# Attention scores computed with the keys on partitions, on one Trainium2 core

## The chip, the cores and the metric

The kernel runs on one core of a Trainium2 chip. A core has five engines that run their own instruction streams and wait for one another through semaphores: TensorE (PE in the profile, its weight loads PEld), VectorE (DVE), ScalarE (ACT), GpSimd (POOL) and SyncE (SP), which here issues all the DMAs. The metric is the device time of one execution in microseconds, the median of several. Before the change it was 720.5 us, the median of three runs (719.56 to 722.37).

## What is computed

One transformer block with cross attention, in fp32. The eight sequences of 256 tokens and 512 features are taken with a context of the same shape; 16 heads of 32 features; an MLP of 2048 inner features. The mask is all ones.

```python
x = layer_norm(hidden_states, ln1_w, ln1_b)
q = (x @ q_w + q_b)                      # -> B, H, LQ, HD
k = (encoder_hidden_states @ k_w + k_b)
v = (encoder_hidden_states @ v_w + v_b)
scores = einsum('bhqd,bhkd->bhqk', q, k) / sqrt(HD)
scores = where(mask, scores, finfo.min)
attn = softmax(scores, axis=-1)
out = einsum('bhqk,bhkd->bhqd', attn, v) @ cproj_w + cproj_b
hidden = out + residual
y = gelu(layer_norm(hidden, ln2_w, ln2_b) @ fc_w + fc_b) @ proj_w + proj_b
return hidden + y
```

## The kernel before

The sequences are worked in two groups of four (`g` = 0, 1). Each projection is a product of 2x2 blocks done with seven products instead of eight (`quad`; the two MLP layers nest this twice, `grown` and `grown2`), so the matrix engine's products alternate with sums and differences of blocks: `plus` and `minus` on DVE or POOL, evictions from PSUM in `take` on ACT or DVE. Results of the projections k, q and v go to DRAM (`kd`, `qd`, `vd`) and come back by unit.

A unit of attention is one sequence and one set of four heads: 32 units. `scores` (L818) loads `ku`, `qu` and `vu`, and issues eight products `s`, 32 rows deep, four heads side by side on the rows of the array. Queries lie on the 128 partitions and 256 keys along the row. For each of the eight tiles of 128x256 a DVE instruction (`max`, L841) adds the mask, scales, writes the tile to `pr` in SBUF and leaves the row's maximum in `st`; an ACT instruction (L847) takes the exponential with that maximum as bias and leaves the row's sum. DVE then takes the reciprocals of the eight sums (L851), transposes them (L854), and two DMAs carry them through DRAM into `r` (`rd`, L505, and back by L499), spread over the 32 partitions of each head. `attend` (L862) runs `LOOK` = 2 units later: 16 transposes of 128x128 on TensorE (`turn`, L870) bring the keys onto partitions, four evictions of 128x512 (`pt`, L512) bring them back to SBUF, eight products `av` multiply by `vu`, and `att` (L532) multiplies by `r` on DVE.

The instruction order of all engines is fixed before anything runs, by a planner in the kernel itself (`Order`). Each operation has a list of engines that can do it with a cost for each (`alts`), and a due time `vt`, worked back from the windows (`WINDOWS`) in which each stream of matrix products is to run. `run` then steps through time and gives every free engine the ready operation with the earliest due time, if a buffer is free. Buffers are slots: `Q` of 1024 columns (two `P` of 512), `H` of 256, PSUM banks `W` for products and `C` for scores and transposes. Operations marked `lock` on DVE and POOL are kept from running at the same time in the plan. DMAs are modelled with a fixed delay and eight lanes. Each engine then executes its list strictly in order.

The streams run in the order: projections of group 0, attention of group 0 (`core0`) mixed with the projections of group 1 and sums of MLP weights (`fw`, `pw`), attention of group 1 (`core1`) mixed with the output projection and the first MLP layer of group 0, and then the output projection of group 1 and the rest of the MLP (`pr0`, `fc1`, `pr1`).

Of the kernel before, what the change touches and what calls it, by code (L numbers as in the profile page):

```python
# [19 lines left out]
FLT_MAX = 3.4028234663852886e38  # L20


SLOTS = {"Q": (45, 1024), "P": (36, 512), "H": (13, 256), "sm": (10, 32), "st": (8, 32), "MB": (4, 256)}
# [3 lines left out]


READY = {"PE": 0.24, "DVE": 0.16, "ACT": 0.18, "POOL": 0.2, "SP": 0.0}
BORROW = 25.6  # L30
SWITCH = 0.0

AHEAD = {"PE": 1000.0, "DVE": 66.7, "ACT": 36.8, "POOL": 25.4, "SP": 26.9}

DMA_FIXED, DMA_RATE, DMA_LANES = 3.0, 0.34, 8
# [10 lines left out]
class Op:  # L46
    __slots__ = (
        "n", "alts", "fn", "deps", "users", "vt", "bufs", "name", "mode", "table", "mb", "start",
        "end", "eng", "stream", "waiting", "ready", "lead", "slack", "psum_of", "after", "lock",
# [3 lines left out]
class Order:  # L53
# [9 lines left out]
    def op(self, name, alts, reads, writes, fn, mode=None, table=None, mb=0.0, lead=0.0, lock=False):  # L63
        o = Op()
        o.n, o.alts, o.fn, o.name, o.mode, o.table, o.mb = (
            len(self.ops), alts, fn, name, mode, table, mb,
        )
        o.lock = lock
        o.deps, o.users, o.vt, o.bufs, o.lead = set(), [], None, [], lead
        o.start = o.end = o.eng = None  # L70
        o.stream, o.psum_of = self.now, None
        o.after = self.streams[self.now][-1] if self.streams[self.now] else None
        for b, keys in reads:
            for k in keys if keys is not None else range(b.keys):
                if k in b.writers:
                    o.deps.add(b.writers[k])
                    if b.kind in BANKS and b.writers[k].alts[0][0] == "PE":
                        o.psum_of = b.writers[k]
                b.readers.setdefault(k, []).append(o)
            if b not in o.bufs:  # L80
                o.bufs.append(b)
        for b, keys in writes:
            for k in keys if keys is not None else range(b.keys):
                if k in b.writers:
                    o.deps.add(b.writers[k])
                for r in b.readers.get(k, []):
                    o.deps.add(r)
# [3 lines left out]
        o.deps.discard(o)  # L91
# [9 lines left out]
    def times(self, windows):  # L101
        pe = lambda o: o.alts[0][0] == "PE"
        for name, ops in self.streams.items():
            if not ops:
                continue
            t0, tm, t1 = windows[name]
            total = sum(o.alts[0][1] for o in ops)
            at = 0.0
            for o in ops:
                f = 2.0 * at / total  # L110
                o.vt = t0 + (tm - t0) * f if f < 1.0 else tm + (t1 - tm) * (f - 1.0)
                at += o.alts[0][1]
        cost = lambda o: min(a[1] for a in o.alts) + READY[o.alts[0][0]] + (
            DMA_FIXED + 1.0 + o.mb / DMA_RATE if o.alts[0][0] == "SP" else 0.0
        ) + o.lead
        for name, (t0, tm, t1) in windows.items():
            back = [o for o in self.ops if o.stream == name and not pe(o)]
            if name not in self.streams or self.streams[name]:
                continue
            for i, o in enumerate(back):  # L120
                o.vt = t0 + (t1 - t0) * i / len(back)
# [3 lines left out]
        for o in reversed(self.ops):  # L125
            if not pe(o):
                c, early = [u.vt for u in o.users], o.vt
                o.vt = (min(c) if c else (o.after.vt if o.after else 0.0) + 20.0) - cost(o)
                if o.psum_of is not None:
                    o.vt = min(o.vt, o.psum_of.vt + 1.2)  # L130
                if early is not None:
                    o.vt = min(o.vt, early)
# [4 lines left out]
    def run(self):  # L137
        ops = self.ops
        free_slots, pending = {}, {}
        for kind, (n, _) in SLOTS.items():  # L140
            free_slots[kind] = [(0.0, i) for i in range(n)]
        for kind, n in BANKS.items():
            free_slots[kind] = [(0.0, i) for i in range(n)]
        pairs = [[0.0, 0.0] for _ in range(SLOTS["Q"][0])]
        free_slots["Q"] = free_slots["P"] = None
        bufs = []
        seen = set()
        for o in ops:
            for b in o.bufs:
                if id(b) not in seen:  # L150
                    seen.add(id(b))
                    bufs.append(b)
        for b in bufs:
            b.left = len(b.ops)
            b.vt = min(o.vt for o in b.ops)
            if b.kind in free_slots:
                pending.setdefault(b.kind, []).append(b)
        for kind in pending:
            pending[kind].sort(key=lambda b: b.vt)
        vts = {kind: [b.vt for b in bs] for kind, bs in pending.items()}  # L160

        light = lambda b: b.kind == "C" and b.name.startswith("ps_") and not b.name.startswith("ps_pt")
        vts["heavy"] = [b.vt for b in pending.get("C", []) if not light(b)]
        engines = ["PE", "DVE", "ACT", "POOL", "SP"]
        at = dict.fromkeys(engines, 0.0)
        cands = {e: [] for e in engines}
        for o in ops:
            o.waiting = len(o.deps)
            o.ready = 0.0
        def offer(o):  # L170
            for e, _ in o.alts:
                cands[e].append(o)
        for o in ops:
            if not o.waiting:
                offer(o)
        port = 0.0
        lanes, n_dma = [0.0] * DMA_LANES, 0
        order, mode, table, lag, dma_at = [], None, None, 0.0, 0.0
        busy = dict.fromkeys(engines, 0.0)
        self.trace = []  # L180

        def room(o, t):

# [1072 lines left out]
```

## Time and profile before

| | |
|---|---|
| median of three runs | 720.5 us (719.56 to 722.37) |
| span of the profiled execution, first to last instruction | 718.6 us |
| instructions | 13,665 |
| TensorE clock granted, mean | 0.997 of full speed |
| moved by DMA | 144.06 MB, 200 GB/s over the span |
| last product `av` of the attention, start | 409.0 us |
| last `att` | 409.5 us, 0.4 us long |

The profiled execution's time apart from its span is not listed; the span lies 1.9 us below the median of the runs. "Busy" is the union of an engine's instructions; on DVE and ACT neighbours overlap by some tens of ns, so the mean length of an instruction is a little more than what it takes from its engine. In a group of instructions the columns are line, engine, operation, output and inputs with their shapes, count, then busy time and mean ns of one, then the idle time of the engine before them and what ended it. In a list of stretches, each engine has its busy microseconds and its number of instructions. In a timeline the columns are start, length, engine, line and operation; an `x3` at the end means that three neighbours are shown as one.

### The profile page before, as it was taken

What the parts mean: (1) busy time and instruction counts of PE and PEld (TensorE: products, weight loads), DVE (VectorE), ACT (ScalarE), POOL (GpSimd) and SP (SyncE); (2) the same over time, 40 slices, a digit from 0 to 9 for tenths busy, and PEclk for the clock granted to TensorE, in tenths of its full rate; (3) what the DMA queues carried; (4) which work ended last, traced back from release to release, by engine and by line L of the source; (5) the groups of instructions that cost most, each with busy time, mean ns of one, the idle gap of its engine ahead of it and who ended that gap; (6) DMA issues with size and microseconds to landing.
All of it is one profiled execution on the core that took longest, in us unless ns stands there. A gap on an engine that the chain in (4) does not pass through costs nothing.

```text
span 718.6 us, 13665 instructions
## 1 busy us (share of the span) xinstructions
PE 699.8 (97%) x4753; PEld 563.0 (78%) x4753; DVE 592.1 (82%) x1382; ACT 294.5 (41%) x829; POOL 281.3 (39%) x261
## 2 busy tenths in 40 slices
PE   6999999998999999999999999999999999998997
PEld 5555675566755687877788799999989988897997
DVE  2889589987898889888988867996579898997992
ACT  2243278657576656745659840120000107610000
POOL 1383046581563700030104588364677004843000
PEclk9999999999999999999999999999999999999999
DMA  7968875998789855274534743468666557730741
GB/s 232 327 205 313 306 252 183 283 337 283 206 281 317 278 183 169 78 219 146 161 94 143 256 123 100 148 204 245 183 180 182 160 157 246 278 103 1 247 150 59
DMA packets 119332, 144.06 MB, mean 200 GB/s; under 512 B 14136, under 2 KB 82272, under 8 KB 119264
## 3 DMA queue, kind: packets, MB, share of 16 engines
q1 hardware_dynamic: 119264, 143.19, 62.7%
q8 instruction: 38, 0.62, 0.4%
q14 instruction: 30, 0.25, 0.1%
HBM read 98.59 MB, written 44.56 MB: 199 GB/s over the span
## 4 chain that ended last, share of the span: by engine, by line
PE 90%; DVE 6%; DMA 2%; issue 1%; SPq 0%; POOL 0%; DVEq 0%; POOLq 0%
PE fc_X L541 13%; PE pr_X L541 13%; PE ps_pt L870 7%; PE fc_W L541 7%; PE pr_W L541 7%; PE s L541 5%; PE av L541 4%; PE k_X L541 4%; PE o_X L541 4%; PE q_X L541 4%; PE v_X L541 3%; PE fc_Y L541 3%; PE pr_Y L541 3%; PE o_W L541 2%; PE q_W L541 2%; PE v_W L541 2%
## 5 line engine op out<-in xcount | busy, mean ns | idle before, releaser
L847 ACT ACTIVATE pr<-pr,st 128x256 f32<-128x256 f32 x256 | 127.4, 502 | 82.3 <-DVE st L841 80.8
L841 DVE CUSTOM_DVE_ANT_0 pr<-s,mb 128x256 f32<-128x256 f32 x256 | 92.4, 418 | 10.1 <-PE s L541 9.9
L1030 ACT ACTIVATE h<-h,cols 128x256 f32<-128x256 f32 x128 | 54.3, 499 | 55.7 <-DVE h L532 52.7
L870 PEld LDWEIGHTS ps_pt<-ident,pr 128*128 128x128 f32 x512 | 59.4, 141 | 18.5 <-issue 5.6
L870 PE MATMUL ps_pt<-ident,pr 128*128 128x128 f32 x512 | 70.1, 275 | 2.4 <-DVE st L841 1.9
L532 DVE TENSOR_TENSOR h<-fc_X,h 128x512 f32<-128x512 f32 x80 | 54.3, 685 | 8.3 <-PE fc_X L541 8.1
L512 ACT COPY pt<-ps_pt 128x512 f32<-128x512 f32 x88 | 49.1, 579 | 24.6 <-PE ps_pt L870 20.5
L847 ACT ACTIVATION_READ_ACCUMULATOR pr<-pr,st 128x1 f32 x256 | 48.9, 191 | 0.0
L532 DVE TENSOR_TENSOR h<-fc_W,h 128x512 f32<-128x512 f32 x48 | 32.9, 686 | 5.3 <-PE fc_W L541 3.7
L541 PE MATMUL s<-ku,qu 32*128 32x256 f32 x512 | 36.9, 400 | 0.0
L541 PE MATMUL av<-pt,vu 128*32 128x256 f32 x512 | 35.0, 385 | 0.0
L541 PEld LDWEIGHTS s<-ku,qu 32*128 32x128 f32 x512 | 23.4, 184 | 13.5 <-issue 12.0
L512 ACT COPY e<-pr_X 128x256 f32<-128x256 f32 x4 | 1.5, 373 | 76.7 <-PE pr_X L541 76.7
L532 POOL TENSOR_TENSOR h<-h,fl 128x512 f32<-128x512 f32 x8 | 11.1, 1396 | 55.5 <-DVE fl L532 54.9
L541 PEld LDWEIGHTS av<-pt,vu 128*32 128x32 f32 x512 | 14.3, 109 | 20.1 <-issue 6.6
L532 DVE TENSOR_TENSOR po<-pr_X,po 128x256 f32<-128x256 f32 x40 | 16.7, 417 | 14.3 <-PE pr_X L541 14.3
L512 DVE COPY pt<-ps_pt 128x512 f32<-128x512 f32 x40 | 26.8, 683 | 1.8 <-PE ps_pt L870 1.1
L841 DVE DVE_READ_ACCUMULATOR2_ANT st<- 128x1 f32 x256 | 21.0, 82 | 0.0
L649 POOL TENSOR_TENSOR rs_y<-rs_y,neg_half 128x2 f32<-128x2 f32 x8 | 6.7, 836 | 35.8 <-DVE rs_y L646 35.7
L530 POOL TENSOR_TENSOR z0t<-h,h 128x512 f32<-128x512 f32 x12 | 15.0, 1272 | 13.3 <-PE fc_X L541 11.6
L530 POOL TENSOR_TENSOR z0i<-z0t,z0t 128x512 f32<-128x512 f32 x10 | 16.4, 1660 | 6.3 <-DVE y1t L532 3.3
L532 DVE TENSOR_TENSOR att<-av,r 128x256 f32<-128x256 f32 x32 | 13.4, 418 | 6.5 <-PE av L541 3.9
(643 smaller groups left out, 1841.7 us busy)
## 6 DMA issues: line engine op xcount, KB each, us to landing
fl<-prd SPq DMA_DIRECT2D x21, 256.0 KB
fl<-fcd SPq DMA_DIRECT2D x19, 256.0 KB
fw<-in_L_xattn_fc_w_dram SPq DMA_DIRECT2D x16, 256.0 KB
ku<-kd SPq DMA_DIRECT2D x32, 128.0 KB
vu<-vd SPq DMA_DIRECT2D x32, 128.0 KB
qu<-qd SPq DMA_DIRECT2D x32, 128.0 KB
r<-rd SPq DMA_DIRECT2D x32, 128.0 KB
pw<-in_L_xattn_proj_w_dram SPq DMA_DIRECT2D x32, 128.0 KB
```

What stands on the lines that cost most here:

```text
L512: (nc.scalar.copy if e == "ACT" else nc.vector.tensor_copy)(to(), of_())
L530: nc.gpsimd.tensor_tensor(to()[:, ts(k, 512)], in0()[:, ts(k, 512)], in1()[:, ts(k, 512)], op)
L532: E[e].tensor_tensor(to(), in0(), in1(), op)
L541: nc.tensor.matmul(o(), l(), r(), start=first, stop=True, skip_group_check=True)
L649: lambda e, rs=rs: nc.gpsimd.tensor_tensor(tile_of(rs)[:, 2:4], tile_of(rs)[:, 0:2], neg_half[:, 0:2], ALU.pow), lock=True)
L841: nc.vector.tensor_tensor_reduce(at(p_, pk), at(sb[j], i), tile_of(mb), scale=-SCALE, scalar=FLT_MAX, op0=ALU.add, op1=ALU.min, accum_out= ...
L847: nc.scalar.activation(at(p_, pk), at(p_, pk), AF.Exp, bias=tile_of(st)[:, 8 + c : 9 + c], scale=-1.0, accum_out=tile_of(st)[:, 16 + c : 1 ...
L870: nc.tensor.transpose(at(ps, 2 * kc + i, 1, P), at(pr[j // 2], 2 * (j % 2) + i)[:, ts(kc, P)], ident.t)
L1030: lambda e, f=f, b=b, c=c: nc.scalar.activation(at(h[f][b], c), at(h[f][b], c), AF.Gelu_apprx_tanh, bias=col(c_fcb + f * 4 + c), scale=1.0 ...
```

## The change

In the new program the scores of a unit come with the keys on partitions: `ku` is loaded into the array and `qu` moves. Nothing is transposed by TensorE. The scale goes into the weight and bias of the first layer norm and the bias of `q`, where `cols` is made, and the mask becomes a bias per partition, so a plain eviction (`take` with a bias, ACT or DVE) brings each of the eight score tiles to `pr`. The maximum over the keys now runs across partitions: two DVE reductions of 128x1024 (`mx`) reduce blocks of 32x32 that they transpose on the way, six small DVE instructions (`fold`) fold the four groups of 32 partitions into one, a DMA stores the 32x32 result to DRAM (`md`), and another brings it to all 128 partitions (`mm`, 128x1024, 512 KB). `less` subtracts it (POOL or DVE, two instructions of 128x512 for each half), ACT takes the exponential of 128x1024, twice per unit, and `ss` adds the two blocks of keys (DVE or POOL, 128x512, twice). `attend` adds four products of `ss` with a tile of ones to the eight of `av`, so that the sums over the keys stand beside the result in the same bank on 32 partitions per head; DVE takes their reciprocal and multiplies.

```diff
-        mm(f"s{u}", 0.97, [(q, None), (k, None)], [(s, None) for s in sb], [
-            (lambda i=i, j=j: at(sb[j], i), lambda i=i, j=j: tile_of(q)[j * HD : (j + 1) * HD, ts(i, P)],
-             lambda j=j: tile_of(k)[j * HD : (j + 1) * HD, :], True)
-            for i in range(2) for j in range(4)], mode="row")
+        row = lambda t, j: tile_of(t)[j * HD : (j + 1) * HD]
+        mm(f"s{u}", 1.076, [(q, None), (k, None)], [(s, None) for s in sb], [
+            (lambda kc=kc, j=j: at(sb[j], kc), lambda kc=kc, j=j: row(k, j)[:, ts(kc, P)], lambda j=j: row(q, j), True)
+            for kc in range(2) for j in range(4)], mode="row")
         pr = [Buf(f"pr{u}_{h}", "Q", 4) for h in range(2)]
-        st = Buf(f"st{u}", "st", 24)
...
-                    nc.vector.tensor_tensor_reduce(
-                        at(p_, pk), at(sb[j], i), tile_of(mb), scale=-SCALE, scalar=FLT_MAX, op0=ALU.add, op1=ALU.min,
-                        accum_out=tile_of(st)[:, 8 + c : 9 + c])
...
+        for kc in range(2):
+            for j in range(4):
+                take(f"ev{u}_{j}{kc}", (pr[j // 2], [2 * (j % 2) + kc]), (sb[j], [kc]), lambda j=j, kc=kc: at(pr[j // 2], 2 * (j % 2) + kc),
+                     lambda j=j, kc=kc: at(sb[j], kc), 256, lambda kc=kc: col(2 * (4 * g + b) + kc))
+        mx = Buf(f"mx{u}", "mx", 3)
+        for h in range(2):
+            T.op(f"mx{u}_{h}", [("DVE", 1.14)], [(pr[h], None)], [(mx, [h])], lambda e, h=h: nc.vector.tensor_reduce(
+                tile_of(mx)[:, 32 * h : 32 * h + 32], tile_of(pr[h]).rearrange("p (n r) -> p n r", r=32), axis=mybir.AxisListType.X,
+                op=ALU.max, apply_transpose=True))
+
+        def fold(e):
+            t = tile_of(mx)
+            part = lambda i, n=P: t[:n, 64 + 32 * i : 96 + 32 * i]
+            two = t[:, 0:64].rearrange("p (j k q) -> p j k q", j=4, k=2)
+            v = nc.vector
+            v.tensor_tensor(part(0).rearrange("p (j q) -> p j q", j=4), two[:, :, 0, :], two[:, :, 1, :], ALU.max)
+            v.transpose(part(1), part(0))
+            v.tensor_copy(part(2, 64), part(1)[64:128])
+            v.tensor_tensor(part(3, 64), part(1, 64), part(2, 64), ALU.max)
+            v.tensor_copy(part(4, 32), part(3, 64)[32:64])
+            v.tensor_tensor(part(5, 32), part(3, 32), part(4, 32), ALU.max)
+        T.op(f"fold{u}", [("DVE", 0.6)], [(mx, [0, 1])], [(mx, [2])], fold)
+        md = dram(f"md{u}", [32, 32])
+        store(f"md{u}", md, None, [(mx, [2])], lambda: md.t, lambda: tile_of(mx)[:32, 224:256], 0.01)
+        M = Buf(f"mm{u}", "Q")
+        load(f"mm{u}", M, None, lambda: tile_of(M), lambda: md.t.rearrange("a r -> (a r)").partition_broadcast(P), 0.5, src=[(md, None)])
+        ss = Buf(f"ss{u}", "Q", 2)
+        for h in range(2):
+            def less(e, h=h):
+                for i in range(2):
+                    j = 2 * h + i
+                    p_ = at(pr[h], i, 1, 512).rearrange("p (k q) -> p k q", k=2)
+                    E[e].tensor_tensor(p_, p_, at(M, j)[:, None, :].to_broadcast([P, 2, S]), ALU.subtract)
+            T.op(f"less{u}_{h}", [("POOL", 2.315), ("DVE", 1.21)], [(pr[h], None), (M, None)], [(pr[h], None)], less, lock=True, pieces=2)
+            T.op(f"exp{u}_{h}", [("ACT", 0.88)], [(pr[h], None)], [(pr[h], None)],
+                 lambda e, h=h: nc.scalar.activation(tile_of(pr[h]), tile_of(pr[h]), AF.Exp), table="exp")
...
-                        nc.tensor.transpose(at(ps, 2 * kc + i, 1, P), at(pr[j // 2], 2 * (j % 2) + i)[:, ts(kc, P)], ident.t)
...
         av = Buf(f"av{u}", "C")
+            (lambda j=j: tile_of(av)[j * HD : (j + 1) * HD, 256:512], lambda: ones, lambda j=j: at(ss, j), True)
+            for j in range(4)] + [
...
+        T.op(f"r{u}", [("DVE", dve(256))], [(av, None)], [(R, None)], lambda e: nc.vector.reciprocal(tile_of(R), tile_of(av)[:, 256:512]))
```

The rest of the change is in the planner and at the start. The planner's model is finer: a delay for each pair of engines (`TAIL`), separate costs for entering and leaving the narrow modes of the array, DMAs with a base and a service time by name, a two-part POOL operation that lets DVE's sums in between its parts (`pieces`), new due times (`WINDOWS`, `LEADS`), and `LOOK` = 3. All instructions of all engines therefore come in another order. At the start, 14 small products on a tile of ones (`WARM`) run on TensorE before any data are there, the context of group 0 is loaded by quarters (`token_quarters`: 256 columns of two row blocks at a time, instead of whole rows), and the masks come as 16 rows beside the bias rows instead of eight broadcasts.

```diff
-LOOK = 2
+LOOK = 3
+WARM = 14
...
+    for _ in range(WARM):
+        nc.tensor.matmul(first[:64, :64], warm, warm, start=True, stop=True, skip_group_check=True)
...
-        ct = token_tiles(g, "c", ef)
+        ct = token_quarters(g, "c", ef) if g == 0 else token_tiles(g, "c", ef)
...
+            halves = o.lock and e == "POOL" and o.pieces == 2
             if o.lock and (e == "DVE" or e == "POOL"):
-                port = t + dur
+                port = t + (dur / 2 if halves else dur)
```

More of the change, by code (lines that the diff above doesn't have):

```diff
@@ L152, in run @@
                     bufs.append(b)
+        light = lambda b: b.name.startswith("ps_") and not b.name.startswith("ps_pt")
+        vts = {k: [] for k in free}
+        vts["heavy"] = []
         for b in bufs:
@@ L155, in run @@
             b.vt = min(o.vt for o in b.ops)
[L156 to L166, printed above, removed]
-        for o in ops:
[L168 to L172, printed above, removed]
+            if b.kind in free:
+                vts[b.kind].append(b.vt)
+                if b.kind == "C" and not light(b):
+                    vts["heavy"].append(b.vt)
+        for v in vts.values():
+            v.sort()
+        at = dict(START)
+        cands = {e: [] for e in ENGINES}
+        for o in ops:
+            o.waiting, o.ready = len(o.deps), 0.0
         for o in ops:
             if not o.waiting:
[L175 to L180, printed above, removed]
+                for e, _ in o.alts:
+                    cands[e].append(o)
+        port, lanes, n_dma, dma_at = 0.0, [0.0] * DMA_LANES, 0, 0.0
+        order, mode, table, lag, second = [], None, None, 0.0, None
+        skip = dict.fromkeys(ENGINES, -1.0)
+        before = lambda k, last: bisect.bisect_left(vts[k], last)
         def room(o, t):
@@ L345, in run @@
[L345 to L353 removed]
+            done(o, o.end + AFTER[e])
+        self.span = max(o.end + AFTER[o.eng] for o in ops)
         return sorted(order, key=lambda o: (o.start, o.n))
```

498 lines of the change are left out of this document (252 added, 246 removed).

## The prediction

> **What bounds the kernel now.** I read the page's busy times first, then its chain of waits, then the busy time of each engine in two stretches, cut at the end of the last attention product (409.9 us).
>
> ```profile
> PE 699.8 (97%) x4753; PEld 563.0 (78%) x4753; DVE 592.1 (82%) x1382; ACT 294.5 (41%) x829; POOL 281.3 (39%) x261
> ...
> PE 90%; DVE 6%; DMA 2%; issue 1%; SPq 0%; POOL 0%; DVEq 0%; POOLq 0%
> ```
>
> ```profile
> core 0: us, PE busy (x) PEld busy (x) DVE busy (x) ACT busy (x) POOL busy (x), PEclk, DMA share, GB/s
> 0.00:18.00 18.00, 11.77 (x54) 9.26 (x55) 5.30 (x7) 4.70 (x7) 2.48 (x16) 1.00 0.71 233
> 0.00:94.30 94.30, 88.02 (x365) 54.90 (x368) 66.06 (x153) 31.75 (x76) 30.91 (x43) 1.00 0.83 279
> ...
> 0.00:409.90 409.90, 400.60 (x2616) 280.45 (x2617) 339.69 (x1006) 244.23 (x717) 147.70 (x166) 1.00 0.71 228
> 409.90:718.60 308.70, 299.16 (x2139) 282.52 (x2137) 252.46 (x378) 50.32 (x113) 133.62 (x96) 0.99 0.53 164
> ```
>
> PE is busy for 400.6 of the first 409.9 us and holds 90% of the chain, so TensorE bounds the attention stage. But DVE is busy for 339.7 us of the same stretch, 83%: there are only 70 us of room on the engine to which the change gives most of its new work. ACT (60%) and POOL (36%) have more. The second stretch holds what the change leaves alone: output projection, MLP, no scores.
>
> **What it takes from TensorE.** These are pieces of the chain, in order of time (start, length, what).
>
> ```profile
> 97.63 1.08 PE s L541 x16
> ...
> 104.49 1.00 PE av L541 x16
> ...
> 108.87 1.75 PE ps_pt L870 x16
> ```
>
> The 16 transposes of one unit cost 1.75 us; 32 units give 56.0 us, all removed. The scores keep shape and count (keys instead of queries are the loaded side), so 1.08 us stays. `av` gains four products with ones to its eight, each of the same moving width: half of 1.00 us more, 16.0 us in all. The issue order of the changed program also puts 24 fc products of 128x256 behind the last `av` that stood ahead of it; the chain has four such products (eight records) in 1.73 us:
>
> ```profile
> 290.13 1.73 PE fc_X L541 x8
> ```
>
> so 10.4 us move from the first stretch to the second. PE's work up to the last `av` is then 400.6 - 56.0 + 16.0 - 10.4 = 350 us. If TensorE still set the pace, the whole would be 718.6 - 56.0 + 16.0 = 678.6 us of span.
>
> **What it gives to DVE.** I count what the changed program issues on DVE up to the last `att`, and price it from start to start, because neighbours overlap by some 0.08 us.
>
> ```profile
> 200.04 0.42 DVE L841 CUSTOM_DVE_ANT_0 pr<-s,mb 128x256 f32<-128x256 f32 x1
> ...
> 201.07 1.29 DVE L512 COPY pt<-ps_pt 128x512 f32<-128x512 f32 x2
> 202.28 0.68 DVE L532 TENSOR_TENSOR xt<-q_Y,xt 128x512 f32<-128x512 f32 x1
> 202.88 2.39 DVE L532 TENSOR_TENSOR x1t<-x,x 128x1024 f32<-128x1024 f32 x1
> 205.19 0.19 DVE L851 RECIPROCAL st<-st 128x8 f32<-128x8 f32 x1
> 205.41 0.21 DVE L854 STREAM_TRANSPOSE tr<-st 128x32 f32<-128x32 f32 x1
> 205.55 0.38 DVE L532 TENSOR_TENSOR att<-av,r 128x256 f32<-128x256 f32 x1
> ```
>
> ```profile
> 450.50 3.49 DVE L532 TENSOR_TENSOR z0t<-h,z0t 128x1024 f32<-128x1024 f32 x3
> 453.90 1.22 DVE L532 TENSOR_TENSOR z0i<-z0t,z0t 128x1024 f32<-128x1024 f32 x1
> ```
>
> Between 200.04 and 201.07 lie three maxima: 0.343 us for 256 columns. Two copies of 512 take 202.28 - 201.07: 0.605 each. Three sums of 1024 take 3.40: 1.133 each. A small instruction that waits for the one before it starts 0.22 us after it (205.41 - 205.19).
> Removed: 256 maxima (87.8), 40 copies of transposed blocks (24.2), 32 reciprocals with their transpose (0.36 each, 11.5), three mask rows (0.8): 124.3 us. The other 88 copies, and the accumulator reads, leave ACT.
> Added: 77 of the 256 evictions with the mask bias (26.4; the other 179 are ACT's); 64 maxima of transposed blocks over 128x1024, at the 1024 price (72.5); 192 instructions of `fold`, six to a unit, each waiting for the one before (42.2); 32 reciprocals of 128x256, at the 0.418 of `att`, since `att` waits for each (13.4); 46 subtractions (27.8) and 29 sums (17.5) of 512. Together 199.8 us. In the rest of DVE's list up to the last `att` some 27 instructions fewer stand there: -13.
> So DVE's work up to the last `att` is 339.7 - 124.3 + 199.8 - 13 = 402 us, against PE's 350. The order of the two has turned round: this is the step on which the forecast rests.
>
> Three prices have no row. The maximum with its transposition may carry the longer tail of the small transpose (0.21 against 0.14 to the next start): at most 0.07 x 64 = 4.5 us more; below 1.133 I see no reason. `fold` could run packed like an accumulator read, 0.082 us, if its waits cost nothing: 192 x 0.082 = 15.7 in place of 42.2. I take 0.22, since a reciprocal and a transpose of the same tile are the same pattern. The third is the meeting with POOL:
>
> ```profile
> 201.66 2.53 POOL L530 TENSOR_TENSOR x1t<-x,x1t 128x512 f32<-128x512 f32 x2
> ```
>
> DVE's `x1t` from 202.88 took 2.39 us, not 1.22: POOL's second half ended at 204.19, and 2.39 is the rest of it and then a full 1.1. So an instruction with two SBUF inputs waits for a POOL instruction in progress. What that costs on the average shows in the groups of such sums:
>
> ```profile
> L532 DVE TENSOR_TENSOR z1t<-h,h 128x1024 f32<-128x1024 f32 x8 | 12.1, 1542 | 0.0
> L532 DVE TENSOR_TENSOR z1t<-h,z1t 128x1024 f32<-128x1024 f32 x8 | 10.2, 1281 | 0.0
> L532 DVE TENSOR_TENSOR z1i<-z1t,z1t 128x1024 f32<-128x1024 f32 x7 | 9.6, 1366 | 0.0
> L1183 DVE TENSOR_TENSOR hid<-hid,pb 128x1024 f32<-128x1024 f32 x7 | 8.5, 1215 | 0.0
> ```
>
> Their weighted mean is 1355 ns against 1215 for the undisturbed: 0.14 us each. The 75 new subtractions and sums add 75 x 0.14 = 11 us at the present share of POOL. Below, nothing, if the new order keeps the two apart; above, the rival on POOL. I take 11.
> [...]
>
> **The sum.** DVE idles for 12.7 of the first 18 us (18.00 - 5.30), before any data are there, and later for
>
> ```profile
> DVE st L851 <- ACT pr L847: 2.8, 5, 1.2
> DVE kws L532 <- DMA ct<-in_L_xattn_k_w_dram: 2.7, 1, 2.7
> DVE att L532 <- DMA r<-rd: 2.6, 1, 2.6
> ```
>
> some 8 us that have nothing to do with PE's pace. I keep both. The first stretch is 402 + 11 + 12.7 + 8 = 434 us; PE sits idle for 84 us of it. The second is 308.7 + 10.4 = 319.1, TensorE's as now, since DVE's load there hardly changes. Span 753. The span of this profile, 718.6, lies 1.9 us under the median of the runs, 720.5; with that, 755 us.
> The start (tokens in quarters, 14 idle products ahead) I price at nothing: it can at most shorten the 6 us for which PE waits for its first tiles, and with DVE ahead in load that does not reach the end in full. ACT's new work (64 exponentials of 1024, 179 evictions) replaces 256 shorter ones with reads and 88 copies, and stays under its 60%.
>
> **The rivals.**
> TensorE stays the bound (faster). For it: a third of the new subtractions alone are DVE's, and DVE can be kept from POOL by order. Against it: even with `fold` packed and no meeting at all DVE needs 402 - 26.5 - 101 x 0.14 = 361 us, plus 20.7 idle: 382, still above 350. That gives 382 + 319.1 + 1.9 = 703 us; TensorE alone gives 678.6 + 1.9 = 681. I take 692. Chance 0.24.
> POOL and DVE block each other (slower still). POOL takes 82 halves of subtractions and 35 sums, at
>
> ```profile
> L530 POOL TENSOR_TENSOR z0t<-h,h 128x512 f32<-128x512 f32 x12 | 15.0, 1272 | 13.3 <-PE fc_X L541 11.6 <-PE pr_W L541 1.5
> ```
>
> 149 us, less 38 us of other sums that leave POOL's list ahead of the last `att` at the same prices: 259 in the stage instead of 147.7, so a meeting is 1.75 times as likely. The 170 long sums and the five instructions of each `fold` that read two inputs or copy in SBUF then lose 330 x 0.14 x 1.75 = 81 us instead of the 25 counted (0.14 for each of 101 + 75): 755 + 56 = 811. It decides once meetings are as frequent as by chance; against it, the planner holds each of the two back while a sum of the other runs, `fold` excepted. Chance 0.14.
> The broadcast comes late. It carries 32 x 512 KB, 12.6 MB more than `r` did; at the 349 GB/s of the fullest stretch that is 36 us of the queue, and it now stands before the exponentials, not behind them. For it:
>
> ```profile
> 59.00:62.00 3.00, 3.00 (x22) 1.48 (x21) 3.00 (x10) 0.69 (x1) 0.00 (x0) 1.00 0.95 349
> ...
> 152.44 7.24 DMA r<-rd
> ```
>
> and DMA busy for 0.83 of the first 94 us. Against it: three units are under way instead of two, some 25 us. If eight units waited 7.24 us each, on a DVE otherwise undisturbed: 703 + 58 = 761. Chance 0.08.
> In between the costs cancel: 720, chance 0.04.
>
> **How the numbers follow.** The forecast, DVE as the bound of the attention stage, has 0.50 and 755 us; its own range, from the low price of `fold` (728) to twenty us more of meetings, is 728 to 775. Faster: 0.24 and a little of the middle, 0.25. Within 0.5%, which is about what these runs can tell from no change: 0.05. Slower: 0.70. The range of 695 to 795 leaves out the better part of the first rival and most of the second, about 2 in 10.
>
> **What would show it.** Right: PE's busy share in the first stretch falls to some 80% with waits for DVE (`pr`, `mx`, `att`), DVE at 95%, the last `av` after 420 us, `fold` near 1.3 us a unit, and about 319 us after the last `av`. Wrong: PE still over 95% before the last `av`, which comes before 390 us; or PE waiting for `mm` DMAs; or POOL instructions of 512 well over 1.27 us.

## The result and the profile after

The changed kernel takes 872.0 us (median of four runs, 869.8 to 876.3), against 720.5 before: 1.210 times as long, with an interval of 1.205 to 1.214. The forecast was 755 us with a range to 795, so the sign was right and the size was not: it is 117 us over the forecast, outside its range. The profiled execution has a span of 871.3 us, and its own time was 873.1.

From the page, the busy times and the shares of the chain of waits (in per cent of the span):

```profile
PE 722.7 (83%) x4525; PEld 545.7 (63%) x4525; DVE 769.2 (88%) x1166; ACT 261.7 (30%) x489; POOL 447.3 (51%) x375
...
PE 29%; DVE 11%; issue 1%; ACT 1%; DMA 1%; POOL 0%; DVEq 0%; SPq 0%
```

The shares add up to 43%, because the chain could be followed back only to 500.2 us. They can't be set beside the 90% before, and they say nothing of most of the attention; from 500.2 to 516.3 us the chain runs along DVE alone. What sets the pace must be read from the stretches and the waits. The stretches, cut at the end of the last `att` (538.1 us; the first `av` starts at 115.7), with the same columns as in the prediction:

```profile
0.00:18.00 18.00, 13.65 (x75) 10.82 (x76) 10.59 (x27) 4.69 (x6) 2.21 (x10) 0.91 0.71 236
0.00:538.10 538.10, 410.79 (x2346) 254.69 (x2347) 498.66 (x801) 188.43 (x325) 291.40 (x259) 0.89 0.61 195
115.70:538.10 422.40, 314.46 (x1954) 196.76 (x1954) 400.68 (x642) 155.48 (x269) 240.15 (x207) 0.88 0.55 173
538.10:871.30 333.20, 311.87 (x2181) 291.03 (x2179) 270.55 (x366) 73.22 (x164) 155.89 (x116) 0.98 0.50 154
```

The first stretch has grown from 409.9 to 538.1 us, the second from 308.7 to 333.2. From the first `av` to the last `att` DVE is busy for 95% of the time (400.68 of 422.40) and TensorE for 74%. The two have changed places as the prediction said; but DVE's list (its busy time up to the last `att`) is 498.7 us long, where 413 were forecast. DVE's groups show where the 86 us are (line, operation, names and shapes, count, then busy us and mean ns of one, and the idle time before them):

```profile
L863 DVE TRANSPOSE_TENSOR_REDUCE mx<-pr 128x32 f32<-128x1024 f32 x64 | 76.9, 1220 | 0.1
L907 DVE RECIPROCAL r<-av 128x256 f32<-128x256 f32 x32 | 55.6, 1739 | 4.7 <-PE av L546 4.7
...
L524 DVE TENSOR_SCALAR pr<-s,cols 128x256 f32<-128x256 f32 x77 | 32.5, 468 | 0.3 <-PE s L546 0.3
L889 DVE TENSOR_TENSOR pr<-pr,mm 128x512 f32<-128x512 f32 x46 | 30.6, 713 | 0.0
L537 DVE TENSOR_TENSOR ss<-pr 128x512 f32<-128x512 f32 x29 | 24.3, 850 | 0.0
L872 DVE TENSOR_TENSOR mx<-mx 128x32 f32<-128x32 f32 x32 | 18.2, 568 | 0.3
...
L875 DVE TENSOR_TENSOR mx<-mx 64x32 f32<-64x32 f32 x32 | 16.0, 499 | 1.1
L876 DVE COPY mx<-mx 32x32 f32<-32x32 f32 x32 | 14.4, 450 | 1.1
L874 DVE COPY mx<-mx 64x32 f32<-64x32 f32 x32 | 14.3, 447 | 1.1
...
L877 DVE TENSOR_TENSOR mx<-mx 32x32 f32<-32x32 f32 x32 | 11.7, 365 | 1.1
...
L873 DVE STREAM_TRANSPOSE mx<-mx 128x32 f32<-128x32 f32 x32 | 6.8, 212 | 1.1
```

Two groups stand out. The reciprocal of 128x256 takes 1739 ns, not 418: 55.6 us instead of 13.4. The six instructions of `fold` add up to 81.4 us instead of 42.2. The transpose among them, which has one input, takes the 0.21 us that was forecast for all; the other five take about twice as much on the average. The list of `mx`'s instructions, with the shortest, the median and the longest in ns, says that this is no fixed price:

```profile
L863 DVE TRANSPOSE_TENSOR_REDUCE mx<-pr x64: 1174/1223/1246, 79.3 to 503.6; 128x32 f32<-128x1024 f32 x64
L872 DVE TENSOR_TENSOR mx<-mx x32: 155/323/1332, 81.7 to 504.8; 128x32 f32<-128x32 f32 x32
L873 DVE STREAM_TRANSPOSE mx<-mx x32: 211/212/215, 81.9 to 506.0; 128x32 f32<-128x32 f32 x32
L874 DVE COPY mx<-mx x32: 176/178/1101, 82.2 to 506.2; 64x32 f32<-64x32 f32 x32
L875 DVE TENSOR_TENSOR mx<-mx x32: 182/183/2269, 82.4 to 507.2; 64x32 f32<-64x32 f32 x32
L876 DVE COPY mx<-mx x32: 169/170/1239, 82.6 to 508.4; 32x32 f32<-32x32 f32 x32
L877 DVE TENSOR_TENSOR mx<-mx x32: 178/180/1198, 82.8 to 509.6; 32x32 f32<-32x32 f32 x32
```

At their shortest the six take 155 + 211 + 176 + 182 + 169 + 178 = 1071 ns, 34.3 us for 32 units. The other 47 us are in a part of them that takes a microsecond longer. One such unit in the timeline (start, length; in brackets the idle time of the engine before it, and the releaser by the profile):

```profile
411.46 0.16 DVE L872 TENSOR_TENSOR mx<-mx 128x32 f32<-128x32 f32 x1
411.66 0.21 DVE L873 STREAM_TRANSPOSE mx<-mx 128x32 f32<-128x32 f32 x1
411.70 4.93 POOL L889 TENSOR_TENSOR pr<-pr,mm 128x512 f32<-128x512 f32 x4 [6.63 <-DVE mx L872]
...
411.90 1.10 DVE L874 COPY mx<-mx 64x32 f32<-64x32 f32 x1
...
413.04 1.20 DVE L875 TENSOR_TENSOR mx<-mx 64x32 f32<-64x32 f32 x1
414.27 1.18 DVE L876 COPY mx<-mx 32x32 f32<-32x32 f32 x1
...
415.48 1.20 DVE L877 TENSOR_TENSOR mx<-mx 32x32 f32<-32x32 f32 x1
```

POOL begins four subtractions, one behind the other, 1.23 us each (4.93 / 4), while DVE runs the transpose. From then on each step of `fold` takes 1.10 to 1.20 us instead of 0.18: it ends when one of POOL's subtractions has ended, and POOL's next is then running before the next step of `fold`, which waits for the one before it, begins. This unit's `fold` becomes 416.68 - 411.46 = 5.2 us long, against 1.27 us for one that meets no POOL instruction (310.16 to 311.43). So in this unit, beside four of POOL's instructions in a row, the short steps of the chain (0.17 to 0.18 us) were held not with the chance of their length, but each of the last four in turn. At least half of all units go free at each of the last four such steps (medians of 170 to 183 ns).

What TensorE waited for, over the whole span, the two largest sums (engine, its tile, the releaser; us in all, times, the longest):

```profile
PE fc_X L546 <- DVE h L537: 17.7, 10, 4.3
PE av L546 <- DVE ss L537: 13.4, 9, 4.7
```

Both are for DVE; the longest single wait is for ACT (9.9 us). TensorE's own time in the first stretch, 411 us, is longer than the 350 of the forecast, but the granted clock there is 0.89. An estimate for full speed is 411 x 0.89 = 366.

### The profile page after: what moved, and what is told of

It reads as the page before. It is cut to its first block, busy times and chain, and to the rows that moved or that the text cites. A ratio compares the mean times of both kernels' runs of the same rounds, so it can differ in the third digit from the quotient of the medians.

```text
span 871.3 us, 12824 instructions
## 1 busy us (share of the span) xinstructions
PE 722.7 (83%) x4525; PEld 545.7 (63%) x4525; DVE 769.2 (88%) x1166; ACT 261.7 (30%) x489; POOL 447.3 (51%) x375
## 5 line engine op out<-in xcount | busy, mean ns | idle before, releaser
L889 POOL TENSOR_TENSOR pr<-pr,mm 128x512 f32<-128x512 f32 x82 | 107.7, 1340 | 61.4 <-DMA mm<-md 48.5
L522 ACT ACTIVATE pr<-s,cols 128x256 f32<-128x256 f32 x179 | 70.5, 479 | 111.2 <-PE s L546 70.9
L892 ACT ACTIVATE pr<-pr 128x1024 f32<-128x1024 f32 x64 | 67.1, 1060 | 78.9 <-POOL pr L889 42.2
L537 POOL TENSOR_TENSOR ss<-pr 128x512 f32<-128x512 f32 x35 | 45.1, 1301 | 69.7 <-ACT pr L892 53.3
L863 DVE TRANSPOSE_TENSOR_REDUCE mx<-pr 128x32 f32<-128x1024 f32 x64 | 76.9, 1220 | 0.1
L907 DVE RECIPROCAL r<-av 128x256 f32<-128x256 f32 x32 | 55.6, 1739 | 4.7 <-PE av L546 4.7
L546 PE MATMUL s<-qu,ku 32*128 32x256 f32 x512 | 47.3, 447 | 7.2 <-DVE att L537 4.3
L546 PE MATMUL av<-ss,ones 128*32 128x256 f32 x256 | 28.5, 433 | 21.8 <-DVE ss L537 13.4
L546 PE MATMUL av<-pr,vu 128*32 128x256 f32 x512 | 44.5, 437 | 0.0
L524 DVE TENSOR_SCALAR pr<-s,cols 128x256 f32<-128x256 f32 x77 | 32.5, 468 | 0.3 <-PE s L546 0.3
L889 DVE TENSOR_TENSOR pr<-pr,mm 128x512 f32<-128x512 f32 x46 | 30.6, 713 | 0.0
```

The source lines that it names most:

```text
L522: nc.scalar.activation(to(), of_(), AF.Identity, bias=bias(), scale=1.0)
L524: nc.vector.tensor_scalar_add(to(), of_(), bias())
L537: E[e].tensor_tensor(to(), in0(), in1(), op)
L546: nc.tensor.matmul(o(), l(), r(), start=first, stop=True, skip_group_check=True)
L863: T.op(f"mx{u}_{h}", [("DVE", 1.14)], [(pr[h], None)], [(mx, [h])], lambda e, h=h: nc.vector.tensor_reduce(tile_of(mx)[:, 32 * h : 32 * h ...
L889: E[e].tensor_tensor(p_, p_, at(M, j)[:, None, :].to_broadcast([P, 2, S]), ALU.subtract)
```

## The experiments

Theory D, in all expectations, is that DVE's list sets the pace up to the last `att`, and that what it lost there is in `r` and in `fold`'s waits for POOL. The rivals are named with each. Every kernel gave one time, but the old attention under the new plan, which was timed four times. The four times of the changed kernel lie 6.5 us apart, so a difference of some 10 us between single times says little.

**The reciprocal alone.**

```diff
-        T.op(f"r{u}", ..., lambda e: nc.vector.reciprocal(tile_of(R), tile_of(av)[:, 256:512]))
+        T.op(f"r{u}", ..., lambda e: nc.vector.tensor_copy(tile_of(R), tile_of(av)[:, 256:512]))
```

> The reciprocal of 128x256, 32 of them at 1739 ns each in the changed kernel, is replaced by a copy of the same tile to the same place; the order of all instructions stays. This leaves out the division by the sums. Theory D: DVE's list sets the pace up to the last att, and what is taken off it comes off the end one for one. The copy should take about 0.4 us, the other 32 x 1.3 = 41 us go: 872 - 41 = 831 us (820 to 845). Theory W: the pace is set elsewhere, by TensorE at a lower granted clock or by the way through DRAM (md, mm) to less and exp, and a shorter r only lengthens DVE's waits: above 860 us.

849.8 us, between the two theories. It goes down by 22, about half of what was removed. Its groups and its first stretch:

```profile
L877 DVE TENSOR_TENSOR mx<-mx 32x32 f32<-32x32 f32 x32 | 16.3, 511 | 1.1
...
L907 DVE COPY r<-av 128x256 f32<-128x256 f32 x32 | 13.1, 409 | 5.3 <-PE av L546 5.3
```

```profile
0.00:515.50 515.50, 408.06 (x2341) 253.80 (x2342) 469.24 (x802) 189.01 (x325) 290.65 (x259) 0.89 0.63 203
```

The copy takes 409 ns, so 42 us went from `r`; DVE's list got only 29 us shorter (498.7 to 469.2), and its idle time 7 us longer (39.4 to 46.3). The missing 13 us came back mostly as waits for POOL: the six groups of `fold` take 91 us in this run, 10 more than in the changed kernel, its last maximum for one at 511 ns instead of 365. D's direction holds, its one for one does not: with a shorter `r`, `fold` was held by POOL for longer.

**`fold` as one instruction.**

```diff
-    SCALE = 1.0 / math.sqrt(HD)
+    SCALE = 0.125 / math.sqrt(HD)
...
-            v.tensor_tensor(part(0)..., two[:, :, 0, :], two[:, :, 1, :], ALU.max)
...
-            v.tensor_tensor(part(5, 32), part(3, 32), part(4, 32), ALU.max)
+            v.tensor_tensor(part(5, 32), t[:32, 0:32], t[:32, 32:64], ALU.max)
```

> The six DVE instructions of fold are replaced by one maximum of 32x32; the order of the rest stays. This leaves out the folding of the four groups of 32 partitions, so the subtracted value is not the true maximum; the scale is an eighth of the true one, so that the exponentials stay finite. In the changed kernel fold took 79.5 us from DVE by the profile (without overlaps), about 36 of work and 43 in waiting for POOL. Theory D: five sixths of it come off the end, 872 - 66 = 806 us; if the waits for POOL only pass to the next DVE instruction with two inputs from SBUF, the work alone, 872 - 30 = 842. Theory W (TensorE's clock or the way through DRAM sets the pace): above 860.

```profile
L872 DVE TENSOR_TENSOR mx<-mx 32x32 f32<-32x32 f32 x32 | 20.6, 645 | 0.3
```

821.9 us, 50 less, between D's two figures. That is more than `fold`'s own work of 34 us, so part of its waits are gone too; but the one instruction that is left takes 645 ns on the average, most of it waiting (the shortest took 155).

**Without POOL's subtractions.**

```diff
             def less(e, h=h):
+                if e == "POOL":
+                    return
                 for i in range(2):
```

The scale is edited as above.

> POOL's share of the subtractions less (41 halves of two instructions) is left out; DVE's share stays, and the order. This leaves out the subtraction of the maximum for these tiles; the scale is an eighth of the true one. POOL's list loses 82 x 1.34 = 108 us. Theory D, with the meetings: DVE loses about 69 us to waits for POOL in its instructions up to the last att, and 82 of some 220 POOL instructions that it can meet are gone: 69 x 82/220 = 26 us off, 872 - 26 = 846 us (830 to 860). Theory W with the way through DRAM and POOL as the bound: POOL waited 48.5 us for mm and ACT 42 us for POOL; as these go for two thirds of the tiles, below 815.

836.5 us, 36 less, though not one DVE instruction was taken out. Its `fold`, in the groups:

```profile
L877 DVE TENSOR_TENSOR mx<-mx 32x32 f32<-32x32 f32 x32 | 10.4, 326 | 1.1
...
L872 DVE TENSOR_TENSOR mx<-mx 128x32 f32<-128x32 f32 x32 | 9.4, 293 | 0.3
...
L875 DVE TENSOR_TENSOR mx<-mx 64x32 f32<-64x32 f32 x32 | 7.8, 245 | 1.1
L874 DVE COPY mx<-mx 64x32 f32<-64x32 f32 x32 | 7.7, 241 | 1.1
...
L876 DVE COPY mx<-mx 32x32 f32<-32x32 f32 x32 | 7.0, 218 | 1.1
L873 DVE STREAM_TRANSPOSE mx<-mx 128x32 f32<-128x32 f32 x32 | 6.8, 212 | 1.1
```

49.1 us instead of 81.4: the 32 us are nearly the whole gain. The time is in D's range. The way through DRAM is not what held the pace of these tiles, for with it gone from two thirds of all tiles the time did not fall below 815.

**The three together.**

> The three edits together: copy for reciprocal, one maximum for fold, no subtractions on POOL. This leaves out the division, the folding and POOL's subtractions; the scale is an eighth. Theory D: 872 - 41 - 66 - 15 (the meetings left after fold is gone) = 750 us, and not below the 681 to 703 at which TensorE becomes the bound. Theory W: above 800, since the lower clock of TensorE and the way md, mm, less (on DVE), exp, ss, av are still there.

```profile
0.00:425.10 425.10, 378.81 (x2341) 239.60 (x2342) 385.45 (x642) 186.18 (x325) 185.55 (x177) 0.94 0.76 246
425.10:759.60 334.50, 313.74 (x2186) 293.23 (x2184) 271.58 (x365) 73.17 (x164) 155.83 (x116) 0.98 0.50 153
```

761.8 us, 110 less; the three alone sum to 22 + 50 + 36 = 108. DVE is still the busiest engine of the stretch (385 against 379), with the same 40 us of idle as in the changed kernel (425.1 - 385.5). With `r` at the forecast's price and the waits out of `fold` the kernel comes to 7 us of the forecast, but partly by luck: its first stretch ends 9 us before the forecast's 434 and its second takes 334.5 us, 15 more than the forecast's. It isn't the forecast's kernel either, since most of `fold`'s work and part of POOL's are left out as well.

**True prices in the planner.** `fold` 0.6 to 1.27, `r` `dve(256)` to 1.70.

> The changed kernel with two prices of its planner set to what the profile shows: reciprocal 1.70 us (planned with the price of a 256-column eviction) and fold 1.27 (planned 0.6); the planner makes the whole order anew. Theory D: the work that only DVE can do stays (evictions apart, mx, fold, r, att), and the planner can only pass a few more sums and evictions to POOL and ACT: 835 to 872 us. Rival P: the loss comes from an order that was made on wrong prices, with the true ones it goes: below 800 us.

874.2 us, 2 above D's range and far from P's: the wrong prices in the plan are not what costs.

**Attention and planner apart.** The new attention under the old planner and start, and the old attention under the new ones:

> The new attention alone (keys on partitions, mx, fold, mm, less, ss, ones, r) under the planner, the windows, LOOK = 2 and the start of the kernel before. Theory D: DVE's list up to the last att is as long as in the changed kernel, so the first stretch stays within 500 to 550 us; the second stretch, which in the changed kernel and in all experiments so far took 329 to 332 us by the last att, against 306 before, goes back to some 306 to 312: 815 to 865 us in all. Rival P (the order of the new planner is what costs): below 780. If the second stretch stays at 330, its 24 us come from the attention.

> The planner, LOOK = 3 and the start of the changed kernel, with the attention of the kernel before (maxima and sums along rows, transposes on TensorE). Theory D: DVE's list is the old one again, TensorE bounds the first stretch at 400 to 415 us; the second stretch keeps the 330 us of the new order: 730 to 748 us. Rival P (the new planner carries the loss): above 780. If the second stretch is 306 again, 705 to 725.

The first took 860.4 us, in D's range (its first stretch 3 us over D's), the second 760.2 (757.1 to 764.6; 1.057 of the time before, interval 1.051 to 1.063). Their stretches, first the new attention, then the old one:

```profile
0.00:553.10 553.10, 429.29 (x2379) 266.28 (x2380) 508.26 (x870) 226.04 (x389) 217.52 (x189) 0.89 0.60 191
553.10:858.60 305.50, 294.76 (x2120) 278.46 (x2118) 258.74 (x378) 56.31 (x125) 125.94 (x88) 1.00 0.54 165
```

```profile
0.00:439.60 439.60, 414.57 (x2617) 281.51 (x2618) 360.14 (x1023) 215.46 (x660) 136.75 (x144) 0.98 0.66 212
439.60:760.00 320.40, 306.58 (x2166) 287.94 (x2164) 256.43 (x361) 69.60 (x160) 147.59 (x112) 0.99 0.51 159
```

| | old planner and start | new planner and start |
|---|---|---|
| old attention | 720 | 760 |
| new attention | 860 | 872 |

So the attention costs 140 us under the old planner and 112 under the new one; the planner costs 40 with the attention that it was not set for, and 12 with the new one (between a single time and a median, so little more than the spread). With the old attention the expectation for the new plan was 730 to 748, and it missed by 12 us: the first stretch came out at 440 us, not 400 to 415, with TensorE busy for 94% of it. The second stretch, 333.2 us in the changed kernel, has 305.5 us with the new attention under the old plan, and 320.4 with the old attention under the new plan; so neither part alone gives the 333.2.

**Without any maximum.** No `mx`, `fold`, `md`, `mm` and `less`; ACT takes the exponential from PSUM:

```diff
-                take(f"ev{u}_{j}{kc}", ...)
+                T.op(f"exp{u}_{j}{kc}", [("ACT", 0.4)], ...,
+                     lambda e, j=j, kc=kc: nc.scalar.activation(at(pr[j // 2], 2 * (j % 2) + kc), at(sb[j], kc), AF.Exp, bias=col(2 * (4 * g + b) + kc), scale=1.0), table="exp")
```

> The changed kernel without any maximum: mx, fold, md, mm and less are left out, ACT takes the exponential from PSUM in tiles of 128x256 with the mask as bias; ss, the products with ones, r and att stay; the scale is an eighth, and the planner makes its order anew. Theory D: DVE's list up to the last att loses the maxima of blocks (73), fold (79) and its subtractions (31), and the evictions (30): 499 - 213 = 286 us, so TensorE becomes the bound again with 350 us of work and some 35 of idle: 385 in the first stretch, 715 us in all (690 to 740). Rival W (the lower clock of TensorE in this stage, or r and ss on the way to av, hold the pace): above 770.

```profile
0.00:426.00 426.00, 375.96 (x2356) 239.79 (x2357) 342.68 (x507) 141.85 (x324) 146.45 (x124) 0.96 0.64 207
```

750.3 us, between the two theories and outside both. DVE falls to 80% of the stretch, as under the old attention, so the maximum over partitions, with the evictions and subtractions that it needs, is what overfilled it. TensorE is the busiest again, at 88%, but the stretch does not come down to the 385 us. The planner, which makes its order anew, gave DVE work that had been POOL's and ACT's: DVE has 507 instructions in the stretch where 422 of the 801 were left, POOL 124 where 177 of the 259 were left. DVE's list came out 57 us longer than the 286 expected. What sets the pace of this kernel was not followed further.

**The reciprocal on ACT.** As exponential of minus the logarithm:

```diff
-        T.op(f"r{u}", [("DVE", dve(256))], ..., lambda e: nc.vector.reciprocal(tile_of(R), tile_of(av)[:, 256:512]))
+        def inverse(e):
+            nc.scalar.activation(tile_of(R), tile_of(av)[:, 256:512], AF.Ln)
+            nc.scalar.activation(tile_of(R), tile_of(R), AF.Exp, scale=-1.0)
+        T.op(f"r{u}", [("ACT", 3.2)], ..., inverse, table="exp")
```

> The changed kernel with its reciprocals on ACT, as the exponential of minus the logarithm of the sums (two activations of 128x256 from PSUM and SBUF for each unit, and two loads of ACT's function tables, since the logarithm is in another one); the planner makes the order anew with 3.2 us of ACT for each. All is computed. Theory D: DVE's list loses 54 us, of which, as with the copy, some 23 come off the end, and up to 54 if the time that r takes no longer stands between DVE's other work: 820 to 850 us. Rival A: ACT, with 32 x 3.2 = 102 us more in the attention stage, and att behind it, is late: 872 or more.

860.7 us, 11 less, outside D's range. The first stretch is not shorter but 10 us longer, and DVE's list there hardly shorter; the gain is all in the second stretch, from which the new order took some 17 us of TensorE's work into the first (311.9 to 295.3):

```profile
0.00:547.90 547.90, 432.44 (x2412) 271.06 (x2413) 488.25 (x824) 280.83 (x414) 302.75 (x273) 0.87 0.60 196
547.90:858.80 310.90, 295.29 (x2114) 278.64 (x2113) 253.64 (x345) 70.86 (x161) 152.81 (x116) 0.99 0.50 157
```

```profile
L524 DVE TENSOR_SCALAR pr<-s,cols 128x256 f32<-128x256 f32 x113 | 47.6, 470 | 4.8 <-PE s L546 4.6
```

```profile
L875 DVE TENSOR_TENSOR mx<-mx x32: 182/652/2277, 86.2 to 507.3; 64x32 f32<-64x32 f32 x32
```

The 54 us of `r` left DVE, but the planner, with ACT fuller, gave DVE work in their place (824 instructions in the stretch instead of 801 in spite of 32 fewer): above all 36 evictions of scores, 113 instead of 77. In `fold` the median of this maximum rose from 183 to 652 ns: about half of the units now meet POOL there. Rival A's figure, 872 or more, was not reached, and ACT has room (281 of 548 us, with the 64 loads of its function tables, 1283 ns each and 82 us in all). So this run shows where the removed work went, not what the reciprocal costs.

**`fold` by TensorE.** One reduction, a turn of 128x32 on TensorE, one reduction from PSUM:

```diff
-        T.op(f"fold{u}", [("DVE", 0.6)], [(mx, [0, 1])], [(mx, [2])], fold)
+        T.op(f"fold{u}", [("DVE", 0.2)], ..., lambda e: nc.vector.tensor_reduce(
+            tile_of(mx)[:, 64:96]..., tile_of(mx)[:, 0:64].rearrange("p (j k q) -> p j q k", j=4, k=2), ..., op=ALU.max))
+        T.op(f"tm{u}", [("PE", 0.11)], ..., lambda e: nc.tensor.transpose(tile_of(tm)[:32, :P], tile_of(mx)[:, 64:96], ident.t), ...)
+        T.op(f"gold{u}", [("DVE", 0.25)], ..., lambda e: nc.vector.tensor_reduce(
+            tile_of(mx)[:32, 224:256], tile_of(tm)[:32, :P].rearrange("n (g c) -> n c g", g=4), ..., op=ALU.max))
```

> The changed kernel with another fold: one DVE reduction with one input (128x32 out of 128x64), a product with the identity on TensorE that turns 128x32 into 32x128, and one DVE reduction of it from PSUM. No step has two inputs from SBUF and none copies inside SBUF. All is computed; the planner makes the order anew. Theory D with the waits for POOL: fold takes 64 x 0.2 = 13 us from DVE instead of 79.5, and the waits that it bore don't all pass on: 815 to 835 us. Rival V: the waits belong to any small DVE instruction between POOL's, or pass on in full, so only 20 us of its own work go: 845 to 872. Rival T: the turn on TensorE stands in its queue behind other products and makes mm late: above 872.

```profile
L867 DVE TENSOR_REDUCE mx<-mx x32: 192/221/224, 80.4 to 462.0; 128x32 f32<-128x64 f32 x32
L873 DVE TENSOR_REDUCE mx<-tm x32: 216/269/279, 82.5 to 465.8; 32x32 f32<-32x128 f32 x32
```

```profile
0.00:490.10 490.10, 406.54 (x2389) 251.19 (x2389) 453.39 (x693) 184.66 (x314) 302.85 (x267) 0.91 0.67 215
```

812.2 us, 60 less (48 of them in the first stretch), with everything computed; a little under D's range. No reduction out of SBUF is longer than 224 ns and none out of PSUM longer than 279, beside a POOL that is busier than in the changed kernel (303 of 490 us, 62%, against 291 of 538): these small reductions were not held by POOL here, so rival V falls. DVE's list is 45 us shorter (498.7 to 453.4), not the 66 by which `fold` became shorter: the new order gives DVE 26 more evictions (11 us), and the same 46 subtractions take 8 us longer. TensorE does wait for the turn's input, 21.8 us by its list of waits, but rival T's loss does not appear.

**Both repairs**, under the new planner and under the old one:

> Both edits together: reciprocals on ACT, fold by TensorE, in the changed kernel; all is computed. Theory D: DVE loses 54 + 66 = 120 us up to the last att, and the two runs before add up: 770 to 805 us. Rival: with DVE's list at 380 us, ACT's tables or TensorE with its lower clock (411 us busy in the stretch) set the pace: 810 to 830.

> Both edits with the new attention under the planner, LOOK = 2 and start of the kernel before (which gave 860 us without the edits, 553 of them up to the last att). All is computed. Theory D: the list of 508 us up to the last att loses 120, so 388 and the same 45 of idle: 433 us, and 306 behind: 739 us; not below 720, since TensorE's work without its transposes is not yet the bound. Rival: as above, TensorE at a lower clock or ACT: 770 to 800.

787.8 us and 796.0. The first is in D's range. The second misses D's 739 by 57 and falls in its rival's range, but DVE is the busiest engine of its first stretch even so: 437.6 of 501.0 us, where 388 of 433 were expected, against 417.7 for TensorE. The first's first stretch:

```profile
0.00:474.40 474.40, 406.39 (x2424) 257.20 (x2425) 424.39 (x690) 280.02 (x418) 319.32 (x274) 0.92 0.70 226
```

Of the 152 us that the change costs, 84 are won back (some 64 in the first stretch, the rest in the second), and the kernel is still 67 us slower than the one before. No version tried beats it.

## Why the prediction was right in sign and wrong in size

| first stretch, us | forecast | measured |
|---|---|---|
| reciprocals of 128x256 | 13.4 | 55.6 |
| `fold` | 42.2 | 81.4 |
| maxima of transposed blocks | 72.5 | 76.9 |
| evictions with the mask bias | 26.4 | 32.5 |
| `less` and `ss` on DVE, with meetings | 45.3 + 11 | 54.9 |
| DVE, all up to the last `att` | 413 | 498.7 |
| DVE idle | 20.7 | 39.4 |
| second stretch | 319.1 | 333.2 |

(The groups' busy times count the overlap of neighbours twice, so the measured rows exceed their part of the list a little.) By the spans, 871.3 us against 753, the miss is 118 us, to rounding: 86 in DVE's list, 19 in its idle time and 14 in the second stretch.

*The bound turns round: right.* DVE at 95% between the first `av` and the last `att`, TensorE waiting for it, the block maximum near the price of an undisturbed sum of 1024 (1220 ns against 1215). `less` and `ss` came near their sum with meetings, but with fewer of them: at their median of 0.68 us the 75 make 51 of the 54.9 us, so the meetings cost some 4, not 11. Every edit that took DVE work or its waits away made the kernel faster, the reciprocal on ACT by no more than 11 us and not in the first stretch; none of them, as long as everything is computed, came below 788.

*The reciprocal: the first mis-sized term.* The step "32 reciprocals of 128x256, at the 0.418 of `att`, since `att` waits for each (13.4)" took the price of a multiplication of the same tile. The row that it had, 0.19 us for a reciprocal of 128x8, is too short to tell a price per column. Measured: 1739 ns, 6.8 ns a column, against 1.6 for the copy (409 / 256). That is 42 us of the forecast's error in DVE's list; with a copy in its place 22 came off the end.

*`fold`: the second.* The step "192 instructions of `fold` ... (42.2)" was near enough for the work, 34.3 us. What failed is the price of a meeting with POOL, "0.14 us each" from the average of long sums, and with it the place where it was put: the 11 us were given to `less` and `ss`, and the meetings of `fold`'s five instructions were left to a rival with a chance of 0.14, at 0.14 x 1.75 = 0.25 us each. On them it was 47 / 160 = 0.29 us. As the timeline shows, POOL's next instruction gets in between two dependent short steps. So the mechanism of "POOL and DVE block each other" came true beside the forecast's, nearly at the rival's price, but mainly on `fold`. This is shown by the run without POOL's subtractions (32 of 81 us gone from `fold`, no DVE instruction removed) and by the one with `fold` by TensorE (48 us off the first stretch). The two copies of `fold`, within SBUF, were held as well (medians 178 and 170 ns, longest 1101 and 1239); that the rival counted them among what POOL can hold was the author's estimate, since before the change all of DVE's copies came from PSUM. The block maxima, which have one input, were not held: median 1223 ns, longest 1246.

*Idle time: 19 us too little.* The start was quicker than forecast (DVE idle for 7.4 of the first 18 us, not 12.7), but DVE waits for 32 us afterwards, not 8. The groups name 4.7 for `av` before `r`, and 1.1 before each of five steps of `fold`, 5.5 in all; the rest is spread over single waits, most of them for products, of which the longest is 2.9 us (`xt` for `v_X`).

*The second stretch: 14 us too little.* The work that moves there was about right: TensorE's busy time grew by 311.9 - 299.2 = 12.7, forecast 10.4. Its idle time grew as well, from 9.5 to 21.3 us, and the step "since DVE's load there hardly changes" did not hold: DVE's busy time grew by 18 us (252.5 to 270.6) with 12 instructions fewer. This belongs to the order more than to the attention: the same attention has 305.5 us there under the old plan, and its variants have 310.9 to 326.7 us in the four orders that the new planner made anew (true prices, reciprocal on ACT, `fold` by TensorE, both repairs), though these also move work across the cut. Why the order of the changed kernel loses there was not tried apart.

*TensorE's 350 us: too low,* but it did not decide. It is 411 us at a clock of 0.89, by the estimate above 366 at full speed; the other 16 us were not followed. In the runs the clock goes with TensorE's busy share, from 0.88 at 74% (115.7 to 538.1 us) over 0.94 at 89% without the three to 1.00 at 98% before the change. The products show it in their lengths: one of `s` takes 374 ns in the median before and after, but the longest is 792 ns instead of 478. That the waits lower the clock is not shown, and whether the low clock costs time by itself was not settled. The start (quarters, idle products) was not run by itself.

*The rivals.* "TensorE stays the bound" and "late broadcast" fell: POOL waited 48.5 us for `mm`, but without that way for two thirds of the tiles the gain, 36 us, is little more than the 32 by which `fold` became shorter.

## What to carry to other kernels

Price an operation only by a row of the same operation at a similar length, and where there is none, time one: here a reciprocal of 128x256 took 1739 ns, a multiplication of 128x256 (`att`) 422. Before moving work to an engine that is 83% busy, see what of it can be held by another engine; here a chain of short dependent instructions, with two inputs or copies within SBUF, could be held by POOL at every step, and paid 0.29 us a step where long sums had paid 0.14. Where something had to be reduced over partitions, reductions with one input and a turn on TensorE kept out of POOL's way (the longest took 224 and 279 ns; 15 us of DVE's time instead of 81).

## What was not expected of the hardware

In the unit shown, a dependent chain on DVE and a queue of instructions on POOL fell into step: 1.10 to 1.20 us for each DVE instruction of 0.18, one for each of POOL's. When `r` was shortened on DVE, `fold` got longer by 10 us, so waits for POOL partly replaced work that was removed. TensorE's granted clock over the first stretch was 0.86 to 0.89 of full speed in the runs where it was busy for 76 to 79% of it, 0.91 to 0.96 at 80 to 89%, and 0.98 to 1.00 at 94% and more. Over the first 18 us alone this does not hold (1.00 at 65% before, 0.91 at 76% after).
